# Turned u halves stored in 2 KB runs and put in order by GpSimd's product in the scans, and bf16 parts turned by TensorE

## The chip, the core and the metric

The kernel runs on one core of a Trainium2 chip. The time is the device time of one launch in microseconds (us), the median of three runs. Engines are named as in the profile: PE is TensorE's matmul (PEld its weight load), DVE is VectorE, ACT is ScalarE, POOL is GpSimd, and SP is SyncE, which here only issues DMAs.

## The reference

Two layers run over 8 images of 128 x 128 points with 128 channels. Layer 0 is linear attention with a layer norm and a residual. Layer 1 is a selective scan in four directions:

```
xb, z = split(x @ Win);  xb = silu(depthwise_conv3x3(xb) + b)          # 256 channels
xf = xb as rows;  xt = xb turned (H and W exchanged)
xs = [xf, reversed xf, xt, reversed xt]                                # u, four directions
dt, Bs, Cs = xs * Wxproj                                               # 8 + 1 + 1 rows
delta = softplus(dt_weight @ dt + bias);  h_l = exp(delta A) h_(l-1) + delta u B_l
y = sum over the directions of (h C_l + u D);  y = y silu(z);  out = norm(y) @ Wout
```

So the convolution's result is needed in two orders, natural and turned, and so are the ten rows of dt, B and C. A scan step needs the product of delta (softplus's result) and u B.

## The kernel before, in words

The launch has three parts, one after the other. Every part's instructions are written in the order in which each engine runs them (`in_order` chains all instructions of one engine, DMA issues on SP's and POOL's queues among them). A late instruction therefore holds up all that is written behind it on its engine.

**Layer 0** (up to about 2,360 us) is not touched by the change.

**layer1_front** (about 2,360 to 4,750 us) makes u. It runs over the images in the order 4, 6, 5, 7, 0, 1, 2, 3, and over each image in 16 steps of 1,024 points (eight lines). One step, `step(n)`, holds for both channel halves: the projection on PE (L478) and its copy by ACT (L487, edges L492), nine taps of the convolution (two on PE, L505; three as scaled copies on ACT, L513, which POOL adds up in two additions, L515; DVE adds the sum, L521, and does four taps, L523), SiLU on ACT into the tile `ures` (L530), the ten rows on PE (L539) and their copy (L543), B spread over the partitions by PE (L551), and the product of u and B on DVE (L560), stored to DRAM in natural order (L561). ACT and POOL sum u D over directions through the DRAM tiles `gts` and `gs` (L583, L586, L593, L605): images 0 and 1 read sums back and add them on POOL (L586), images 6, 7, 2, 3 issue two accumulating DMAs a step on POOL's queue (L605), images 4 and 5 only store.

The turned order comes from `ures`, eight steps later. `turn` (L617 or L627) copies 16 columns by 64 lines of `ures`, turned, into a tile `turned` (128 x 1,024 values); there are two copies a step, ka at the step's start and kb at its end, 256 in all. `copy_on` chooses the engine of each: DVE for 48 of them, by `dve_copy`, a scalar_tensor_tensor x * 1.0 max x that reads the tile twice (L627), POOL for 134, ACT for 69, and the tail's five plain copies on DVE. `store_turned` (L624) stores each to the DRAM tile `ubs[b, TURN]`. A full turned line has 128 values and the tile holds half of each, so a store has 2,048 runs of 256 B.

The ten rows of an image are loaded back two at a time during the next image (`load_rows`, L644), turned in fp32 by PE (L650) and copied by ACT (L652); both orders are then split into three bf16 parts each (`split`, which calls `split3`: three casts L44 and two subtractions L46; the casts on DVE are L627). The splits run on DVE while images 0 and 1 are in work, else on POOL. `store_parts` (L666) stores the parts to `xps`. After the last step a tail makes the last turned copies and splits.

**layer1_scan** (from 4,750 us) runs 8 groups of 4 slots of 16 units, 512 units of 1,024 points. Groups with o % 4 < 2 read the turned u, the others the natural one: 256 units each. One unit n, `step(n)`: `load_rows` (L934, L935) and `load` of u B for both channel halves (1 MB, L941), `delta` on PE (L952), `soften` on ACT (softplus from PSUM into `sp`, L956), `decay` on ACT (exp, L960), `weigh` on POOL (u B times softplus, in place in u's tile `ubt`, L963), `scan` on DVE (L971, L973, in place in `ubt`; its start value is the last column of the unit before), then `emit` on DVE (times C, L991, L994, L1001, L1005), `gather` on DVE (L1013) and `add` on POOL (two additions of 128 x 512, L1021). While a group's result leaves (slots 4, 8, 12 and so on of 32, and the end), the gate, norm and output projection run in between. `load(n + 3)` stands at the end of step n, because the tile it fills is free only then; `ubt` has four buffers of 8 KB a partition and `sp` two of 4 KB.

The lines that a sentence can't say, in the kernel before:

```
dst = ubs[b, TURN][c].rearrange("p (h w) -> p h w", w=W)
nc.sync.dma_start(dst[:, 16 * i : 16 * i + 16, hf * HALF : hf * HALF + HALF], turned.pop(k))
...
nc.gpsimd.tensor_tensor(ubt[n][:, c, :], ubt[n][:, c, :], sp.pop((n, c)), ALU.mult)
```

Of the kernel before, what the change touches and what calls it, by code (L numbers as in the profile page):

```python
# [8 lines left out]
F32 = mybir.dt.float32  # L9
# [28 lines left out]
NAT, TURN = 0, 1  # L38


def split3(eng, parts, x, copy):

    for j in range(3):
        copy(parts[j], x)  # L44
        if j < 2:
            eng.tensor_tensor(x, x, parts[j], ALU.subtract)  # L46

# [336 lines left out]
def layer1_front(ctx: ExitStack, tc, x1, win, conv_w, conv_b, wxp, d_par, ubs, xds, xps, gts, gs):  # L384
# [76 lines left out]
    def place_of(n):  # L461
        return SEQ[n // NCH % B], n % NCH
# [156 lines left out]
    def store_turned(k):  # L619
        m, r = divmod(k, COPIES)  # L620
        b, hf = SEQ[m // 2], m % 2
        c, i = divmod(r, COPIES // NC2)
        dst = ubs[b, TURN][c].rearrange("p (h w) -> p h w", w=W)
        nc.sync.dma_start(dst[:, 16 * i : 16 * i + 16, hf * HALF : hf * HALF + HALF], turned.pop(k))  # L624

    def dve_copy(out, x):
        nc.vector.scalar_tensor_tensor(out, x, 1.0, x, ALU.mult, ALU.max)  # L627

    def copy_on(n, second):
        s = place_of(n)[0] // 2 if n < N else 2  # L630
        if s == 0:
            return nc.scalar.copy if second else dve_copy if n % 2 else nc.gpsimd.tensor_copy
        if s % 2 == 1 and second:
            return dve_copy if n % 2 else nc.scalar.copy
        return nc.gpsimd.tensor_copy

    NROW = R + 2
    xws, parts = {}, []

    def load_rows(q, r0, rows, tag, bufs):  # L640
        x = wp.tile([P, rows, H], F32, name="xw", tag=tag, bufs=bufs)
        xws[q, r0] = x
        src = xds[SEQ[q]].rearrange("r (w h) -> w r h", h=H)
        nc.sync.dma_start(x, src[:, r0 : r0 + rows, :])  # L644

    def turn_rows(q, r0, rows, tag, bufs):
        x = xws[q, r0]
        pt = (pm if rows <= 4 else pj).tile([P, rows, P], F32, name="ptx", tag="m" if rows <= 4 else "pj")
        for j in range(rows):
            nc.tensor.transpose(pt[:, j, :], x[:, j, :], ident)  # L650
        y = wp.tile([P, rows, W], F32, name="xh", tag=tag, bufs=bufs)
        nc.scalar.copy(y, pt)  # L652
        xws[q, r0, TURN] = y

    def split(q, r0, rows, order, eng, tag, bufs):
        v = xws.pop((q, r0, TURN) if order == TURN else (q, r0))
        p = wp.tile([P, 3, rows, P], BF16, name="parts", tag=tag, bufs=bufs)
        split3(eng, [p[:, j] for j in range(3)], v, dve_copy if eng is nc.vector else eng.tensor_copy)
        parts.append((q, r0, rows, order, p))

    def store_parts():
        while parts:
            q, r0, rows, order, p = parts.pop()
            dst = xps[SEQ[q], order].rearrange("j r (a e) -> a j r e", e=P)
            for j in range(3):
                nc.sync.dma_start(dst[:, j, r0 : r0 + rows, :], p[:, j])  # L666

    def split_step(n):

        q, d = divmod(n - 2, NCH)  # L670
        q -= 1
        j, odd = divmod(d, 2)
        if not 0 <= q < B or n >= N or d > NROW:
            return
        eng = nc.vector if place_of(n)[0] // 2 == 0 else nc.gpsimd
        if odd:
            turn_rows(q, 2 * j, 2, "sy", 1)
            split(q, 2 * j, 2, NAT, eng, "sq", 1)
        else:
            if j:  # L680
                split(q, 2 * j - 2, 2, TURN, eng, "sq", 1)
            if 2 * j < NROW:
                load_rows(q, 2 * j, 2, "sx", 1)

    def step(n):

        live, then, later, before = 0 <= n < N, 0 <= n + 1 < N, 0 <= n + 2 < N, 1 <= n <= N
        b, g = place_of(n)
        ka, kb = 2 * (n - 8) - 1, 2 * (n - 8)
        if live:  # L690
            taps_dve(n, 0)
        if ka >= 0:
            turn(ka, copy_on(n, False), "tc", 2)
        if before:
            add_sum(n - 1)
        if before:
            keep_rows(n - 1)
        if live:
            taps_pe(n, 1)
        if later:  # L700
            load(n + 2)
        if then:
            project(n + 1, 1)
            taps_act(n + 1, 0)
            place(n + 1, 1)
        store_parts()
        if before:
            store_sum(n - 1)
        if live:
            for c in range(NC2):  # L710
                load_sum(n, c)
        if ka - 1 >= 0:
            store_turned(ka - 1)
        if before:
            for hf in range(2):
                spread(n - 1, hf)
        if live:
            silu(n, 0)
        if then:
            taps_pe(n + 1, 0)  # L720
        if later:
            project(n + 2, 0)
        if live:
            taps_dve(n, 1)
        if then:
            taps_act(n + 1, 1)
        if ka >= 0:
            store_turned(ka)
        if before:
            by_b(n - 1)  # L730
        if live:
            silu(n, 1)
        if later:
            place(n + 2, 0)
        if live:
            rows(n)
            sum_d(n)
        if kb >= 0:
            turn(kb, copy_on(n, True), "tc", 2)
        split_step(n)  # L740

    def tail():

        store_parts()
        q, k0 = B - 1, 2 * (N - 8)
        store_turned(k0)
        for i in range(2):
            load_rows(q, 5 * i, 5, "d", 2)
        for k in range(k0 + 1, 2 * B * COPIES):
# [2 lines left out]
            turn(k, copy, "tc" if i % 3 == 2 else "tb", 2 if i % 3 == 2 else 4)  # L752
            store_turned(k)
        for i in range(2):
            turn_rows(q, 5 * i, 5, "tb", 4)
            for order in (TURN, NAT):
                split(q, 5 * i, 5, order, nc.vector, "tb", 4)
                store_parts()

    with in_order(tc):  # L760
        for n in range(-2, N + 1):
# [5 lines left out]
def layer1_scan(ctx: ExitStack, tc, ubs, xps, zs, gs, dtw, dtb, a_log, gamma, beta, w_out, out):  # L767
# [34 lines left out]
    wparts = dram.tile([3, R, K, D2], BF16, name="wparts")  # L802
    bparts = dram.tile([3, K, D2], BF16, name="bparts")
    for dst, src, rows in ((wparts, dtw.rearrange("k r d -> r k d"), R), (bparts, dtb.rearrange("o (k d) -> o k d", d=D2), 1)):
        x = wp.tile([rows, K, D2], F32, name="w32", tag="sp", bufs=2)
        nc.sync.dma_start(x, src)
        q = wp.tile([rows, 3, K, D2], BF16, name="w16", tag="ub", bufs=4)
        split3(nc.vector, [q[:, j] for j in range(3)], x, nc.vector.tensor_copy)
        for j in range(3):
            if rows == 1:  # L810
                nc.sync.dma_start(dst[j : j + 1], q[:, j])
            else:
                nc.sync.dma_start(dst[j], q[:, j])
# [123 lines left out]
    def load(n):  # L937
        sl, i = units[n]
        m = sl.at(i)
        ubt[n] = wp.tile([P, NC2, CH], F32, name="ubt", tag="ub", bufs=4)  # L940
        nc.sync.dma_start(ubt[n], ubs[sl.b, sl.order].rearrange("c p l -> p c l")[:, :, m * CH : m * CH + CH])  # L941

    def delta(n, c):
        sl, i = units[n]
# [7 lines left out]
            nc.tensor.matmul(p[:, hf * 512 : hf * 512 + 512], sl.dw[:, c * P : c * P + P], src, start=True, stop=True)  # L952

    def soften(n, c):
        sp[n, c] = t = wp.tile([P, CH], F32, name="sp", tag="sp", bufs=2)
        nc.scalar.activation(t, da[n, c], AF.Softplus)  # L956

    def decay(n, c):
        sl, i = units[n]
        nc.scalar.activation(da[n, c], sp[n, c], AF.Exp, scale=sa[:, sl.s, c : c + 1])  # L960

    def weigh(n, c):
        nc.gpsimd.tensor_tensor(ubt[n][:, c, :], ubt[n][:, c, :], sp.pop((n, c)), ALU.mult)  # L963

    def scan(n, c):
        sl, i = units[n]
        x, e = da[n, c], ubt[n][:, c, :]
        last = 0 if sl.back else CH - 1
        start = 0.0 if i == 0 else ubt[n - 1][:, c, last : last + 1]
# [11 lines left out]
    def emit(n, hf):  # L981
# [1 line left out]


        sl, i = units[n]
        h = ubt[n][:, :, hf * 512 : hf * 512 + 512]
        c = cps.pop((n, hf)).to_broadcast([P, NC2, GN])
        if sl.place == 0:
            v = sl.y_at(i, hf)
# [25 lines left out]
    def add(n):  # L1015
        sl, i = units[n]
        hf = 1 - sl.first
        h = ubt[n][:, :, hf * 512 : hf * 512 + 512].rearrange("p c (a b) -> p c a b", b=H)
        v = sl.y_at(i, hf)
        for c in range(NC2):  # L1020
            nc.gpsimd.tensor_tensor(v[:, c], v[:, c], h[:, c], ALU.add)  # L1021
# [95 lines left out]
    def step(n):  # L1117
# [49 lines left out]
        if live:  # L1167
            scan(n, 1)
        if first:
            ubt.pop(n - 1)  # L1170
            if n + 3 < N:
                load(n + 3)
        if now:
            variance(now[1])
        if live:
# [16 lines left out]
            da.pop((n, 1))  # L1192
        if before and not first:
            add(n - 1)
            ubt.pop(n - 1)
        if n + 3 < N and not first:
            load(n + 3)
        if n in weighed:
            units[weighed[n]][0].weights()
        if n in summed:  # L1200
# [2 lines left out]
    with in_order(tc):  # L1203
        for n in range(2):
            units[n * NCH][0].weights()
        for n in range(2):
            load_rows(n)
        for n in range(3):
            load(n)
# [5 lines left out]
    assert not da and not ubt and not zt  # L1215


@with_exitstack
# [61 lines left out]
```

## Time and profile before

| | |
|---|---|
| median of three runs | 9462.86 us (9462.46 to 9480.5) |
| profiled execution | 9477.74 us; its span, first to last instruction, is 9475.9 us |
| layer 0, front, scans in that span | 0 to 2,360, 2,360 to 4,751, 4,751 to 9,476 us |
| busy shares over the span | DVE 86%, POOL 79%, ACT 75%, PE 67% |
| DMA | 1,784 MB in 1,510,245 packets, 799,444 of them under 512 B |

How to read the profile: a row of the group view names line, engine, operation, output <- inputs, the shapes and the count; behind the bar come busy time and the mean of one in ns, then the engine's idle time before the group and what ended it. The windows view gives each engine's busy time in a stretch with its instructions (x), and at the end of the row PE's granted clock, the share of time in which the 16 DMA engines were busy, and GB/s. "SPq" is SP's queue, where a row's time is that of the issue, not of the transfer.

### The profile page before, as it was taken

The page shows a single profiled execution, that of the slowest core. Times are in us where ns is not written, and L with a number is a line of the kernel's source. Part 1 is how long each engine was busy: PE and PEld are TensorE (multiplying, and loading weights), DVE is VectorE, ACT ScalarE, POOL GpSimd, SP SyncE. Part 2 cuts the span into 40 slices and gives each one's busy share as a digit, 9 for nine tenths or more (in the row PEclk, how much of TensorE's full clock was granted, in tenths as well). Part 3 has the DMA queues.
Part 4 walks back from the last instruction along what each step waited for, and adds up shares of the span by engine and source line. Part 5 has one row for each costly group of instructions (what it writes and reads, how often), then busy time and mean ns, then how long its engine had stood idle before and what let it go on. Part 6 is the DMA issues. An engine that isn't in the chain of part 4 may idle for free. (4 is left out here: it accounts for less than half of the span.)

```text
span 9475.9 us, 89695 instructions
## 1 busy us (share of the span) xinstructions
PE 6389.1 (67%) x24352; PEld 3122.5 (33%) x24352; DVE 8149.5 (86%) x8046; ACT 7125.4 (75%) x8034; POOL 7474.3 (79%) x4743
## 2 busy tenths in 40 slices
PE   8999999898989887788633644637345363543636
PEld 5555555564333332233200311304023040320403
DVE  6667765563999999999789999999999999999996
ACT  5556655567888887788678888888878888888884
POOL 3445544455789987788769999999999999999997
PEclk9999999999999998899855755758566585665857
DMA  2331233314598898999955958769586685967858
GB/s 92 134 134 71 106 134 132 133 63 152 180 230 244 231 231 229 233 232 224 226 158 171 273 154 228 223 181 264 158 238 203 190 256 166 247 187 201 248 163 214
DMA packets 1510245, 1784.08 MB, mean 188 GB/s; under 512 B 799444, under 2 KB 1025364, under 8 KB 1501552
## 3 DMA queue, kind: packets, MB, share of 16 engines
q1 hardware_dynamic: 1456496, 1577.01, 53.5%
q0 software_dynamic: 53248, 201.34, 11.4%
q8 instruction: 199, 3.26, 0.1%
q14 instruction: 302, 2.47, 0.1%
HBM read 1085.92 MB, written 692.12 MB: 188 GB/s over the span
## 5 line engine op out<-in xcount | busy, mean ns | idle before, releaser
L963 POOL TENSOR_TENSOR ubt<-ubt,sp 128x1024 f32<-128x1024 f32 x1024 | 2458.0, 2458 | 160.0 <-ACT sp L956 96.1
L952 PE MATMUL px<-rows,dtw 128*128 128x512 bf16 x2048 | 953.6, 565 | 2238.4 <-DVE y L1013 1069.2
L515 POOL TENSOR_TENSOR tap<-tap 128x1024 f32<-128x1024 f32 x512 | 1261.4, 2468 | 234.3 <-ACT tap L513 209.2
L523 DVE SCALAR_TENSOR_TENSOR acc<-xb,cw,acc 128x1024 f32<-128x1024 f32 x1024 | 1320.6, 1290 | 54.0 <-ACT xb L492 1.7
L956 ACT ACTIVATE sp<-px 128x1024 f32<-128x1024 f32 x1024 | 1046.2, 1024 | 418.1 <-PE px L952 351.0
L1021 POOL TENSOR_TENSOR y<-y,ubt 128x512 f32<-128x512 f32 x768 | 1155.3, 1550 | 146.0 <-DVE ubt L994 144.9
L505 PE MATMUL acc<-xi,wt 128*128 128x512 f32 x2048 | 1028.1, 648 | 314.3 <-ACT ures L530 314.3
L973 DVE TENSOR_TENSOR_SCAN ubt<-px,ubt 128x1024 f32<-128x1024 f32 x512 | 1176.9, 2332 | 27.4 <-POOL ubt L963 20.3
L971 DVE TENSOR_TENSOR_SCAN ubt<-px,ubt 128x1024 f32<-128x1024 f32 x512 | 1178.4, 2332 | 13.1 <-POOL ubt L963 6.0
L952 PEld LDWEIGHTS <-dtw 128*128 128x128 bf16 x2048 | 164.6, 109 | 3065.9 <-issue 869.7
L960 ACT ACTIVATE px<-sp,sa 128x1024 f32<-128x1024 f32 x1024 | 1110.1, 1109 | 6.1
L513 ACT ACTIVATE tap<-xb,cw 128x1024 f32<-128x1024 f32 x768 | 828.3, 1140 | 134.9 <-DVE acc L521 85.4
L282 POOL TENSOR_TENSOR q<-q,qs 128x512 f32<-128x512 f32 x256 | 271.7, 1061 | 698.2 <-DVE qs L281 698.2
L956 ACT ACT_TABLE_LOAD x512 | 656.9, 1283 | 169.6 <-PE px L952 146.9
L505 PEld LDWEIGHTS acc<-xi,wt 128*128 128x128 f32 x2048 | 398.1, 205 | 917.6 <-issue 497.1
L960 ACT ACT_TABLE_LOAD x512 | 656.9, 1283 | 9.0
L1086 PEld LDWEIGHTS px<-wg,z 128*128 128x128 f32 x4096 | 556.6, 219 | 117.9 <-issue 112.7
L979 PE MATMUL pc<-rows,csel 128*128 128x512 bf16 x1024 | 515.8, 584 | 81.3 <-DVE rstd L1074 77.5
L1086 PE MATMUL px<-wg,z 128*128 128x128 f32 x4096 | 556.7, 302 | 0.0
L478 PE MATMUL pxb<-xi,wi 128*128 128x512 f32 x1024 | 483.7, 595 | 10.1 <-DMA xi<-x 7.9
L1013 DVE TENSOR_TENSOR y<-y,px 128x1024 f32<-128x1024 f32 x384 | 468.7, 1221 | 14.4
L298 ACT ACTIVATE sq<-o 128x512 f32<-128x512 f32 x256 | 161.2, 630 | 420.1 <-DVE o L296 418.9
(160 smaller groups left out, 15379.7 us busy)
## 6 DMA issues: line engine op xcount, KB each, us to landing
ubt<-ubs SPq DMA_DIRECT2D x512, 1024.0 KB
zs<-z SPq DMA_DIRECT2D x512, 256.0 KB
ubs<-ures SPq DMA_DIRECT2D x256, 512.0 KB
ubs<-turned SPq DMA_DIRECT2D x256, 512.0 KB
z<-zs SPq DMA_DIRECT2D x256, 512.0 KB
y<-gs POOLq DMA_DIRECT2D x128, 1024.0 KB, 10.4
rows<-xps SPq DMA_DIRECT2D x1536, 60.0 KB
xi<-x SPq DMA_DIRECT2D x120, 576.0 KB
```

The lines of the kernel that those rows point to most:

```text
L505: nc.tensor.matmul(acc[:, s, :], wt[:, j, c, :], x, start=(j == 0), stop=(j == len(ON_PE) - 1))
L513: nc.scalar.activation(t, at(n, c, *d), AF.Copy, scale=cw[:, c, tap(*d) : tap(*d) + 1])
L515: nc.gpsimd.tensor_tensor(sums[n, c], sums[n, c], t, ALU.add)
L523: nc.vector.scalar_tensor_tensor(acc, at(n, c, *d), cw[:, c, tap(*d) : tap(*d) + 1], acc, ALU.mult, ALU.add)
L952: nc.tensor.matmul(p[:, hf * 512 : hf * 512 + 512], sl.dw[:, c * P : c * P + P], src, start=True, stop=True)
L956: nc.scalar.activation(t, da[n, c], AF.Softplus)
L960: nc.scalar.activation(da[n, c], sp[n, c], AF.Exp, scale=sa[:, sl.s, c : c + 1])
L963: nc.gpsimd.tensor_tensor(ubt[n][:, c, :], ubt[n][:, c, :], sp.pop((n, c)), ALU.mult)
L971: nc.vector.tensor_tensor_scan(e[:, ::-1], x[:, ::-1], e[:, ::-1], start, ALU.mult, ALU.add)
L973: nc.vector.tensor_tensor_scan(e, x, e, start, ALU.mult, ALU.add)
L1021: nc.gpsimd.tensor_tensor(v[:, c], v[:, c], h[:, c], ALU.add)
L1086: nc.tensor.matmul(po[:, w, :], z[:, c, w * H : w * H + H], wg[:, c, :], start=(c == 0), stop=(c == NC2 - 1))
```

## The change

Four edits.

1. `store_turned` writes the tile as it lies: a chunk of 1,024 points of `ubs[b, TURN]` now holds two half blocks (columns 0 to 63 of eight lines, then columns 64 to 127), each one run of 2 KB. A store has 256 runs of 2 KB in place of 2,048 of 256 B.
2. `weigh` multiplies from `ubt` into softplus's tile `sp`; for turned units it reads `ubt` by a view of 8 lines by 2 halves by 64 columns, which restores the order. `scan`, `emit` and `add` then work in `sp`, which becomes three buffers of both halves (8 KB), while `ubt` becomes four buffers of one half (4 KB); `load(n + 2, c)` is issued per half, right behind `weigh(n, c)`.
3. The rows are split first (natural order only) and the three bf16 parts are turned by PE (six transposes with a bf16 identity in place of two fp32 ones), copied by ACT and stored.
4. No copy or split of the steps runs on DVE: the 48 copies go to POOL (134 to 170) and ACT (69 to 81), and all splits but the tail's to POOL. A copy on ACT stands at the end of the step; a copy on POOL stands where ka and kb stood.

```
-        dst = ubs[b, TURN][c].rearrange("p (h w) -> p h w", w=W)
-        nc.sync.dma_start(dst[:, 16 * i : 16 * i + 16, hf * HALF : hf * HALF + HALF], turned.pop(k))
+        dst = ubs[b, TURN][c].rearrange("p (g e q) -> p g e q", e=2, q=8 * HALF)[:, 2 * i : 2 * i + 2, hf, :]
+        nc.sync.dma_start(dst, turned.pop(k).rearrange("p (g h) w -> p g (h w)", g=2))
...
         if s == 0:
-            return nc.scalar.copy if second else dve_copy if n % 2 else nc.gpsimd.tensor_copy
-        if s % 2 == 1 and second:
-            return dve_copy if n % 2 else nc.scalar.copy
-        return nc.gpsimd.tensor_copy
+            late = n % 2 == 0 if second else n % 8 != 0
+        else:
+            late = s % 2 == 1 and second and n % 2 == 1
+        return nc.scalar.copy if late else nc.gpsimd.tensor_copy
...
+    def split(q, r0, rows, eng, tag, bufs):
+        p = wp.tile([P, 3, rows, P], BF16, name="parts", tag=tag, bufs=bufs)
+        split3(eng, [p[:, j] for j in range(3)], xws[q, r0])
+        xws[q, r0] = p
+        parts.append((q, r0, rows, NAT, p))
+
+    def turn_parts(q, r0, rows, tag, bufs):
+        p = xws.pop((q, r0))
+        pt = (pm if rows <= 2 else pj).tile([P, 3, rows, P], BF16, name="ptx", tag="m" if rows <= 2 else "pj")
+        for j in range(3):
+            for r in range(rows):
+                nc.tensor.transpose(pt[:, j, r, :], p[:, j, r, :], ident16)
+        y = wp.tile([P, 3, rows, P], BF16, name="xh", tag=tag, bufs=bufs)
         nc.scalar.copy(y, pt)
+        parts.append((q, r0, rows, TURN, y))
...
-        eng = nc.vector if place_of(n)[0] // 2 == 0 else nc.gpsimd
         if odd:
-            turn_rows(q, 2 * j, 2, "sy", 1)
-            split(q, 2 * j, 2, NAT, eng, "sq", 1)
+            split(q, 2 * j, 2, nc.gpsimd, "sq", 1)
         else:
             if j:
-                split(q, 2 * j - 2, 2, TURN, eng, "sq", 1)
+                turn_parts(q, 2 * j - 2, 2, "sy", 1)
...
     def soften(n, c):
-        sp[n, c] = t = wp.tile([P, CH], F32, name="sp", tag="sp", bufs=2)
-        nc.scalar.activation(t, da[n, c], AF.Softplus)
+        if c == 0:
+            sp[n] = wp.tile([P, NC2, CH], F32, name="sp", tag="sp", bufs=3)
+        nc.scalar.activation(sp[n][:, c, :], da[n, c], AF.Softplus)
...
     def weigh(n, c):
-        nc.gpsimd.tensor_tensor(ubt[n][:, c, :], ubt[n][:, c, :], sp.pop((n, c)), ALU.mult)
+        u, t = ubt.pop((n, c)), sp[n][:, c, :]
+        if units[n][0].order == TURN:
+            u = u.rearrange("p (e h w) -> p h e w", e=2, w=W // 2)
+            t = t.rearrange("p (h e w) -> p h e w", e=2, w=W // 2)
+        nc.gpsimd.tensor_tensor(t, u, t, ALU.mult)
...
             weigh(n, 0)
+            if n + 2 < N:
+                load(n + 2, 0)
...
             weigh(n, 1)
+            if n + 2 < N:
+                load(n + 2, 1)
```

More of the change, by code (lines that the diff above doesn't have):

```diff
@@ L38, with split3 @@
 NAT, TURN = 0, 1
-def split3(eng, parts, x, copy):
+def split3(eng, parts, x):
     for j in range(3):
-        copy(parts[j], x)
+        eng.tensor_copy(parts[j], x)
         if j < 2:
@@ L412, in layer1_front @@
     make_identity(nc, ident)
+    ident16 = const.tile([P, P], BF16, name="ident16")
+    nc.vector.tensor_copy(ident16, ident)
     cw = const.tile([P, NC2, 9], F32, name="cw")
@@ L622, in store_turned @@
         c, i = divmod(r, COPIES // NC2)
-        dst = ubs[b, TURN][c].rearrange("p (h w) -> p h w", w=W)
-        nc.sync.dma_start(dst[:, 16 * i : 16 * i + 16, hf * HALF : hf * HALF + HALF], turned.pop(k))
-    def dve_copy(out, x):
-        nc.vector.scalar_tensor_tensor(out, x, 1.0, x, ALU.mult, ALU.max)
+        dst = ubs[b, TURN][c].rearrange("p (g e q) -> p g e q", e=2, q=8 * HALF)[:, 2 * i : 2 * i + 2, hf, :]
+        nc.sync.dma_start(dst, turned.pop(k).rearrange("p (g h) w -> p g (h w)", g=2))
     def copy_on(n, second):
@@ L640, in load_rows @@
     def load_rows(q, r0, rows, tag, bufs):
-        x = wp.tile([P, rows, H], F32, name="xw", tag=tag, bufs=bufs)
-        xws[q, r0] = x
+        xws[q, r0] = x = wp.tile([P, rows, H], F32, name="xw", tag=tag, bufs=bufs)
         src = xds[SEQ[q]].rearrange("r (w h) -> w r h", h=H)
         nc.sync.dma_start(x, src[:, r0 : r0 + rows, :])
[L646 to L651, printed above, removed]
-        nc.scalar.copy(y, pt)
[L653 to L659, printed above, removed]
+    def split(q, r0, rows, eng, tag, bufs):
[10 more added lines that the diff above has]
+        y = wp.tile([P, 3, rows, P], BF16, name="xh", tag=tag, bufs=bufs)
+        nc.scalar.copy(y, pt)
+        parts.append((q, r0, rows, TURN, y))
     def store_parts():
         while parts:
-            q, r0, rows, order, p = parts.pop()
+            q, r0, rows, order, p = parts.pop(0)
             dst = xps[SEQ[q], order].rearrange("j r (a e) -> a j r e", e=P)
@@ L691, in step @@
             taps_dve(n, 0)
-        if ka >= 0:
-            turn(ka, copy_on(n, False), "tc", 2)
+        late = []
+        for k, second in ((ka, False), (kb, True)):
+            if k >= 0 and copy_on(n, second) == nc.scalar.copy:
+                late.append(k)
+        if ka >= 0 and ka not in late:
+            turn(ka, nc.gpsimd.tensor_copy, "tc", 2)
         if before:
@@ L711, in step @@
                 load_sum(n, c)
-        if ka - 1 >= 0:
-            store_turned(ka - 1)
+        for k in sorted(turned):
+            if k != ka:
+                store_turned(k)
         if before:
@@ L726, in step @@
             taps_act(n + 1, 1)
-        if ka >= 0:
+        if ka in turned:
             store_turned(ka)
@@ L737, in step @@
             sum_d(n)
-        if kb >= 0:
-            turn(kb, copy_on(n, True), "tc", 2)
+        for k in (ka, kb):
+            if k in late:
+                turn(k, nc.scalar.copy, "tc", 2)
+            elif k == kb >= 0:
+                turn(k, nc.gpsimd.tensor_copy, "tc", 2)
         split_step(n)
@@ L745, in tail @@
         q, k0 = B - 1, 2 * (N - 8)
-        store_turned(k0)
+        for k in sorted(turned):
+            store_turned(k)
         for i in range(2):
@@ L754, in tail @@
         for i in range(2):
[L755 to L758, printed above, removed]
+            split(q, 5 * i, 5, nc.vector, "tb", 4)
+            turn_parts(q, 5 * i, 5, "tb", 4)
+        store_parts()
     with in_order(tc):
@@ L804, in layer1_scan @@
     for dst, src, rows in ((wparts, dtw.rearrange("k r d -> r k d"), R), (bparts, dtb.rearrange("o (k d) -> o k d", d=D2), 1)):
-        x = wp.tile([rows, K, D2], F32, name="w32", tag="sp", bufs=2)
+        x = wp.tile([rows, K, D2], F32, name="w32", tag="sp", bufs=3)
         nc.sync.dma_start(x, src)
-        q = wp.tile([rows, 3, K, D2], BF16, name="w16", tag="ub", bufs=4)
-        split3(nc.vector, [q[:, j] for j in range(3)], x, nc.vector.tensor_copy)
+        q = wp.tile([rows, 3, K, D2], BF16, name="w16", tag="sp", bufs=3)
+        split3(nc.vector, [q[:, j] for j in range(3)], x)
         for j in range(3):
@@ L935, in load_rows, with load @@
         nc.sync.dma_start(rw[96:99, :], xps[sl.b, sl.order, :, R + 1, m * CH : m * CH + CH])
-    def load(n):
+    def load(n, c):
         sl, i = units[n]
         m = sl.at(i)
-        ubt[n] = wp.tile([P, NC2, CH], F32, name="ubt", tag="ub", bufs=4)
-        nc.sync.dma_start(ubt[n], ubs[sl.b, sl.order].rearrange("c p l -> p c l")[:, :, m * CH : m * CH + CH])
+        ubt[n, c] = wp.tile([P, CH], F32, name="ubt", tag="ub", bufs=4)
+        nc.sync.dma_start(ubt[n, c], ubs[sl.b, sl.order, c][:, m * CH : m * CH + CH])
     def delta(n, c):
@@ L954, in soften @@
     def soften(n, c):
-        sp[n, c] = t = wp.tile([P, CH], F32, name="sp", tag="sp", bufs=2)
-        nc.scalar.activation(t, da[n, c], AF.Softplus)
+        if c == 0:
+            sp[n] = wp.tile([P, NC2, CH], F32, name="sp", tag="sp", bufs=3)
+        nc.scalar.activation(sp[n][:, c, :], da[n, c], AF.Softplus)
     def decay(n, c):
         sl, i = units[n]
-        nc.scalar.activation(da[n, c], sp[n, c], AF.Exp, scale=sa[:, sl.s, c : c + 1])
+        nc.scalar.activation(da[n, c], sp[n][:, c, :], AF.Exp, scale=sa[:, sl.s, c : c + 1])
     def weigh(n, c):
-        nc.gpsimd.tensor_tensor(ubt[n][:, c, :], ubt[n][:, c, :], sp.pop((n, c)), ALU.mult)
+        u, t = ubt.pop((n, c)), sp[n][:, c, :]
[3 more added lines that the diff above has]
+        nc.gpsimd.tensor_tensor(t, u, t, ALU.mult)
     def scan(n, c):
         sl, i = units[n]
-        x, e = da[n, c], ubt[n][:, c, :]
+        x, e = da[n, c], sp[n][:, c, :]
         last = 0 if sl.back else CH - 1
-        start = 0.0 if i == 0 else ubt[n - 1][:, c, last : last + 1]
+        start = 0.0 if i == 0 else sp[n - 1][:, c, last : last + 1]
         if sl.back:
@@ L985, in emit @@
         sl, i = units[n]
-        h = ubt[n][:, :, hf * 512 : hf * 512 + 512]
+        h = sp[n][:, :, hf * 512 : hf * 512 + 512]
         c = cps.pop((n, hf)).to_broadcast([P, NC2, GN])
@@ L1017, in add @@
         hf = 1 - sl.first
-        h = ubt[n][:, :, hf * 512 : hf * 512 + 512].rearrange("p c (a b) -> p c a b", b=H)
+        h = sp[n][:, :, hf * 512 : hf * 512 + 512].rearrange("p c (a b) -> p c a b", b=H)
         v = sl.y_at(i, hf)
@@ L1169, in step @@
         if first:
-            ubt.pop(n - 1)
-            if n + 3 < N:
-                load(n + 3)
+            sp.pop(n - 1)
         if now:
@@ L1194, in step @@
             add(n - 1)
-            ubt.pop(n - 1)
-        if n + 3 < N and not first:
-            load(n + 3)
+            sp.pop(n - 1)
         if n in weighed:
@@ L1207, in layer1_scan @@
             load_rows(n)
-        for n in range(3):
-            load(n)
+        for n in range(2):
+            for c in range(NC2):
+                load(n, c)
         for c in range(NC2):
@@ L1214, in layer1_scan @@
             step(n)
-    assert not da and not ubt and not zt
+    assert not da and not ubt and not sp and not zt
 @with_exitstack
```

## The prediction

> **What bounds the kernel now.** I read the windows view first, one row per image of the front, then two slots of the scans, to see which engine is full in which stage. Layer 0 (to 2,360 us) is untouched.
>
> ```profile
> core 0: us, PE busy (x) PEld busy (x) DVE busy (x) ACT busy (x) POOL busy (x), PEclk, DMA share, GB/s
> 2381.00:2626.00 245.00, 227.90 (x568) 87.49 (x568) 235.16 (x190) 219.82 (x239) 181.87 (x84) 0.99 0.61 195
> 2626.00:2906.00 280.00, 241.03 (x595) 92.60 (x592) 260.46 (x201) 236.55 (x254) 247.91 (x167) 0.97 0.94 229
> 2906.00:3156.00 250.00, 230.10 (x580) 88.79 (x578) 238.34 (x193) 217.22 (x240) 236.63 (x152) 0.99 0.83 249
> ...
> 3445.00:3779.00 334.00, 251.52 (x574) 96.86 (x572) 316.69 (x251) 243.90 (x251) 268.19 (x107) 0.88 0.90 232
> ...
> 5028.00:5160.00 132.00, 46.46 (x97) 10.86 (x96) 129.71 (x82) 108.62 (x97) 125.49 (x65) 0.50 0.57 176
> 5293.00:5472.00 179.00, 142.59 (x978) 101.22 (x971) 169.06 (x215) 145.69 (x158) 162.94 (x88) 0.92 0.94 277
> ```
>
> DVE is fullest everywhere. Images 4 and 5 (rows 1 and 3) have no turned copy on DVE and take 245 and 250 us, 15.3 to 15.6 a step. Image 6 (row 2) has DVE copies in its odd steps and takes 280; images 7, 2, 3 take 289, 291, 282. Image 0 (row 4), with the splits on DVE too, takes 334, image 1 338. The group view of image 6 and the timeline around a copy show why:
>
> ```profile
> L523 DVE SCALAR_TENSOR_TENSOR acc<-xb,cw,acc 128x1024 f32<-128x1024 f32 x128 | 165.1, 1290 | 6.6
> L521 DVE TENSOR_TENSOR acc<-tap,acc 128x1024 f32<-128x1024 f32 x32 | 39.1, 1221 | 0.0
> L560 DVE TENSOR_TENSOR ures<-ures,pb 128x1024 f32<-128x1024 f32 x33 | 38.7, 1214 | 0.0
> L627 DVE SCALAR_TENSOR_TENSOR turned<-ures 128x1024 f32<-128x1024 f32 x8 | 23.4, 2920 | 13.0 <-DMA ubs<-turned 13.0
> ```
>
> A copy costs DVE 2.9 us and, on average over these eight, 1.6 us of waiting for the store that frees its tile. Those stores are the many small packets:
>
> ```profile
> DMA packets 108837, 64.10 MB, mean 229 GB/s; under 512 B 76202, under 2 KB 95786, under 8 KB 108823
> ```
>
> In the scans an ordinary unit takes 132/16 = 8.2 us, with DVE at 98% and POOL at 95%. The timeline shows DVE going from scan to emit without a gap and POOL about 2.5 us ahead of it:
>
> ```profile
> 5069.15 4.58 DVE L973 TENSOR_TENSOR_SCAN ubt<-px,ubt 128x1024 f32<-128x1024 f32 x2
> 5069.31 3.22 POOL L1021 TENSOR_TENSOR y<-y,ubt 128x512 f32<-128x512 f32 x2 [0.40 <-DVE ubt L994]
> ```
>
> **The front, by engine and step (16 steps an image), after the change.**
>
> DVE: 8 x 1.290 + 2 x 1.222 + 2 x 1.214 = 15.2 us, in every image. Copies and splits are gone from it.
>
> ACT without copies: 6 taps x 1.140 (L513) + 2 x 1.109 (L530) + 2 x 1.007 (L487) + 2 x 0.407 (L492) + 0.572 (L543) + 2 x 1.140 (L583, L593) = 14.74. A copy is 1.99 (L617). The copy of turned parts reads 128x768; the rows 355 ns at 128x256 and 692 at 128x640 (L652) give 0.8 us, five an image, 0.25 a step. Images 6, 7, 2, 3 copy in every second step: 14.74 + 1.0 + 0.25 = 16.0. Images 0 and 1 make 44 copies in 32 steps: 14.74 + 2.74 + 0.25 = 17.7.
>
> POOL: four additions x 2.41 (L515, third image) = 9.64. A natural split is 3 x 0.40 + 2 x 0.67 = 2.54 us (L44, L46), five an image, 0.79 a step; the turned splits vanish. A copy is 2.00 (L617). Images 6, 7, 2, 3: 9.64 + two DMA issues 2.03 (L605) + 1.5 copies 3.0 + 0.79 = 15.5. Images 0 and 1: 9.64 + 2 x 2.88 (L586) + 10/16 x 2.0 + 0.79 = 17.4. Image 5: 9.64 + 4.0 + 0.79 = 14.4.
>
> PE: 36 matmuls a step as now, plus bf16 transposes in place of fp32 ones: 240 for 80 over the whole front. The nearest rows, 300 ns for an fp32 transpose (L650), bound the 160 extra at 48 us over 128 steps beside PE's idle 7 to 25%; I take nothing.
>
> DMA: in the packet records of image 6 a 256 B packet holds an engine for 18 ns and a 2 KB packet for 84 to 89. A turned store thus falls from 2,048 x 18 / 16 = 2.3 us of all 16 engines to 256 x 89 / 16 = 1.4, or 1.8 us less a step. Image 6's DMA work of 0.94 x 17.5 = 16.4 a step becomes 14.7, image 0's 0.90 x 20.9 = 18.8 becomes 17.0. Both stay under ACT, image 0 barely.
>
> So ACT becomes the fullest engine, at 16.0 and 17.7 us, with DVE and POOL close behind. A stage does not reach its fullest engine's sum. Against the sums of DVE's durations now, image 4 takes 1% over 15.2, image 5 3%, images 0 and 1 3 to 4.5% over 20.2 (15.2, eight copies of 3.2 an image and five double splits of some 11 us), and image 6 5% over 16.65 (15.2 and eight copies of 2.92), store waits included. I take 3.5%: 16.55 x 16 = 265 for images 6, 7, 2, 3; 18.35 x 16 = 294 for 0 and 1; 247 for image 5; 245 for image 4. The sum is 4 x 265 + 2 x 294 + 247 + 245 = 2,140 against 2,309 (2,381 to 4,690): **-170 us**. At 1% it would be -211, at 6.5% -120. Moving the copies to ACT is free only while DVE's slack covers it: ACT's late copies stand ahead of L543's copy of the rows, for which PE's spread of B (L551) and then DVE's L560 wait, 2 us later in images 0 and 1. DVE needs that at the end of its step, so several us of cover remain.
>
> **Tail.** From 4,690 us to the first scan at 4,783 SP issues 15 turned stores in one 35 us row (2.3 us each, which is the packet price), then DVE makes 20 split operations of 0.82 us. The stores shrink by 15 x 0.9 = 13 us. Ten split operations go (8 us); transposes and two copies of 128x1920 (1.8 us each by the same line) add about 4. I take **-15**, bounds -6 (stores no faster) and -24.
>
> **Scans.** DVE's operations are the same, in other tiles. Three sp buffers let softplus of unit n+1 start once `add(n-2)` is done, one step earlier than needed; ACT's softplus waits for PSUM now (L956 on PE px L952, 337 us in this stage), so nothing follows. The loads move from the end of scan n to behind `weigh(n)`, and are needed two units later: about 14 us of lead in place of 15, against some 6 us from the first load's issue to POOL's first product. The new waits stand on SP's queue; behind them stand the stores of r and the next unit's rows, and weigh(n) ends before the scan that both follow, so I cost that at nothing. The first product waits for half a load: -2.
>
> The product's new view is not in the trace. Below, it could cost nothing more, and nothing in the change makes it cheaper than today's 2.37 us. Above, L586 reads one operand with a 32 B step: 2.88 against 2.37, +0.51; worse is the addition L1021 in turned slots, 1.62 against 1.26 per 512 values, +0.73 per 1,024, with two operands at 512 B steps. Nearest is L282: 16 runs of 32 values beside a broadcast take 1.05 per 512, no more than the plain 1.26. The new view has runs of 64, so I take 0.
>
> [...]
>
> **Sum.** -170 - 15 - 2 = -187 on the profiled execution's 9477.7, so 9290. The median lies 15 below that execution; the forecast is 9290 - 15 = 9275.
>
> **Rivals.**
> - The three full engines couple worse, as copies come in bursts (up to 4 us of ACT's time in an even step of images 0 and 1): 10% over the fullest sum, 17.6 and 19.5 a step, front -64, in all about 9380. For it: ACT, POOL, DMA and DVE are all within 2 us. Against: image 5 runs at 3% with POOL at 95%.
> - The stores are no cheaper in 2 KB runs (the change doesn't do what it says): DMA stays at 0.94, so 17.5 a step in images 6, 7, 2, 3, and 18.8 / 0.94 = 20 in 0 and 1; -28, tail -6: 9430. Against: the 2 KB packets' own 84 ns.
> - The product costs +0.51, as L586. An ordinary unit has 0.35 us of POOL's time left, the units of leaving slots about 1.0, slot 0 more. 12 ordinary turned slots x 16 x (1.02 - 0.35) + little in three leaving ones = 130: 9405.
> - **Slower**: the product is priced like the turned addition, +0.73. POOL then bounds the turned units: 192 x (1.46 - 0.35) + 48 x (1.46 - 1.0) = 235 us against 187 saved, 9275 + 235 = 9510. It decides where 480 products' extra less 115 us of slack eats the 187, at +0.63, a product of about 3.0 us.
>
> **How the numbers follow.** Forecast 0.72 (own range 9208 at 1%, tail -24 and 20 more from SP's shorter queue; 9337 at 6.5% and tail -6); coupling 0.10; stores 0.05; product +0.51 0.06; slower 0.07. The range reaches to the coupling case: 9205 to 9385, which leaves out 0.18. A measurement of this kernel tells about 0.2% (19 us) from no change; 9430 is 33 under, so part of that case counts as same: faster 0.90, same 0.03, slower 0.07.
>
> **What would show it.** Right: images 6, 7, 2, 3 at 260 to 270 us and 0 and 1 at 285 to 300, ACT above 95% there; packets under 512 B down by 524,288; the tail row of stores near 21 us; the product at 2.37 us in turned slots and an ordinary unit at 8.2. Wrong: DVE idle for PE acc L505 behind ACT (coupling), a DMA share still at 0.94, or turned slots longer than natural ones.

## The result and the profile after

The changed kernel takes 10,189.99 us (median of four runs, 10,178.22 to 10,196.01) where the kernel before takes 9,468.54 on the same chip: 1.0759 times as long, 95% interval 1.074 to 1.0777. The profiled execution took 10,178.22 us, its span is 10,176.4.

| us | before | after | forecast | measured |
|---|---|---|---|---|
| layer 0, to the front's first tap | 2,381 | 2,374 | 0 | -7 |
| front | 2,309 | 2,284 | -170 | -26 |
| tail | 93 | 72 | -15 | -21 |
| scans | 4,693 | 5,447 | -2 | +754 |

The front begins with DVE's first work on an image and ends with its last product of u and B; the scans run from the first scan to the span's end. Layer 0 is untouched: over all the traces here it differs by some 10 us. The windows view of after, with rows for images 4, 6, 5 and 0, the slot of the scans ahead of the first one in which a group leaves, and that leaving slot:

```profile
2374.00:2620.00 246.00, 228.91 (x570) 87.88 (x570) 235.32 (x191) 219.91 (x239) 181.82 (x85) 0.99 0.56 195
2620.00:2894.00 274.00, 235.13 (x600) 89.26 (x596) 239.00 (x192) 231.64 (x250) 237.01 (x149) 0.98 0.85 228
2894.00:3145.00 251.00, 234.10 (x610) 90.99 (x610) 239.12 (x194) 223.08 (x245) 226.65 (x128) 0.99 0.74 254
3421.00:3756.00 335.00, 262.96 (x607) 99.42 (x608) 240.51 (x193) 263.93 (x267) 267.56 (x136) 0.89 0.84 236
5182.00:5335.00 153.00, 47.39 (x105) 11.98 (x109) 131.35 (x80) 108.80 (x97) 128.72 (x76) 0.50 0.72 187
5335.00:5549.00 214.00, 167.31 (x985) 122.78 (x978) 161.78 (x216) 148.24 (x159) 148.95 (x88) 0.78 0.82 232
```

The slot ahead of the leaving one, before:

```profile
5160.00:5293.00 133.00, 47.03 (x103) 11.19 (x107) 129.22 (x81) 109.89 (x98) 127.29 (x75) 0.50 0.79 211
```

Read the rows against those of before. In image 6 DVE's work fell from 260 to 239 us and the DMA share from 0.94 to 0.85, as the change meant them to, but the image lost only 6 us: now PE, DVE, ACT and POOL are all at 85 to 87%. In image 0 DVE fell from 317 to 241 and the image did not get shorter at all. In the slot of the scans DVE and POOL have nearly the work they had, yet it grew from 133 to 153 us and both stand idle for 14 to 16% of it. (A slot with no work of a leaving group beside it grew from 131.5 to 151.2; the seven leaving slots grew from 180 to 215 on average, 245 of the 754 us.) Where every engine has room and the time is still spent, one suspects a chain that closes from one step to the next.

The group view names the first such chain:

```profile
L974 POOL TENSOR_TENSOR sp<-ubt,sp 128x1024 f32<-128x1024 f32 x1024 | 2393.5, 2358 | 1179.7 <-ACT px L967 555.9
...
L984 DVE TENSOR_TENSOR_SCAN sp<-px,sp 128x1024 f32<-128x1024 f32 x512 | 1191.3, 2345 | 406.1 <-POOL sp L974 406.0
```

POOL's product takes 2.36 us (2.46 before), in natural and turned slots alike, so the new view costs nothing. But POOL stands idle for 1,180 us ahead of it, 556 of them until ACT's exp (L967), and the scans wait for the product for 406 + 399 us (26 before). The timeline of one unit shows the loop (rows between left out; a row's idle time stands in brackets):

```profile
5266.67 4.66 DVE L984 TENSOR_TENSOR_SCAN sp<-px,sp 128x1024 f32<-128x1024 f32 x2 [1.08 <-POOL sp L974]
...
5269.08 1.03 PE L958 MATMUL px<-rows,dtw 128*128 128x512 bf16 x2 [3.56 <-DVE sp L984]
...
5270.15 1.02 ACT L963 ACTIVATE sp<-px 128x1024 f32<-128x1024 f32 x1 [2.24 <-PE px L958]
...
5271.19 1.28 ACT L967 ACT_TABLE_LOAD   x1
...
5272.49 2.15 ACT L967 ACTIVATE px<-sp,sa 128x1024 f32<-128x1024 f32 x2
...
5273.75 2.34 POOL L974 TENSOR_TENSOR sp<-ubt,sp 128x1024 f32<-128x1024 f32 x1 [1.24 <-DMA rows<-xps]
```

The row of scans is two of 2.33 us. The first ends at 5269.0 and frees a PSUM buffer (`px`, which PE writes); PE fills it for the next unit, ACT makes softplus, loads exp's table and makes two exps; the product starts 0.16 us after the first exp's end (5272.49 + 1.10), and the next scan starts with the product's end, at 5276.12: 9.45 us a unit, and 16 x 9.45 = 151. The exp reads `sp`, and the product now writes `sp`, so it may not start until that exp has read. Before, the product wrote into `ubt`, and exp and product both only read softplus's tile. The bracket's releaser ("rows<-xps") is inferred; the times say more. In after none of the 1,024 products starts before the exp of its tile has ended; in before 1,023 of them did, by 3.1 us in the median.

### The profile page after: what moved, and what is told of

The parts are those of the page before. It is cut to its first block, busy times and chain, and to the rows that moved or that the text cites. A ratio compares the mean times of both kernels' runs of the same rounds, so it can differ in the third digit from the quotient of the medians.

```text
span 10176.4 us, 89797 instructions
## 1 busy us (share of the span) xinstructions
PE 6528.0 (64%) x24512; PEld 3233.5 (32%) x24512; DVE 7907.9 (78%) x7889; ACT 7150.0 (70%) x8046; POOL 7323.3 (72%) x4704
## 5 line engine op out<-in xcount | busy, mean ns | idle before, releaser
L974 POOL TENSOR_TENSOR sp<-ubt,sp 128x1024 f32<-128x1024 f32 x1024 | 2393.5, 2358 | 1179.7 <-ACT px L967 555.9
L958 PE MATMUL px<-rows,dtw 128*128 128x512 bf16 x2048 | 981.5, 580 | 2927.8 <-DVE y L1024 1022.7
L963 ACT ACTIVATE sp<-px 128x1024 f32<-128x1024 f32 x1024 | 1047.2, 1023 | 945.3 <-PE px L958 939.9
L984 DVE TENSOR_TENSOR_SCAN sp<-px,sp 128x1024 f32<-128x1024 f32 x512 | 1191.3, 2345 | 406.1 <-POOL sp L974 406.0
L982 DVE TENSOR_TENSOR_SCAN sp<-px,sp 128x1024 f32<-128x1024 f32 x512 | 1192.5, 2345 | 399.0 <-POOL sp L974 398.7
L517 POOL TENSOR_TENSOR tap<-tap 128x1024 f32<-128x1024 f32 x512 | 1212.8, 2371 | 276.5 <-ACT tap L515 256.2
L1032 POOL TENSOR_TENSOR y<-y,sp 128x512 f32<-128x512 f32 x768 | 1150.2, 1529 | 0.0
L967 ACT ACTIVATE px<-sp,sa 128x1024 f32<-128x1024 f32 x1024 | 1109.9, 1109 | 6.1
L1097 PEld LDWEIGHTS px<-wg,z 128*128 128x128 f32 x4096 | 623.5, 240 | 84.2 <-issue 74.7
L1097 PE MATMUL px<-wg,z 128*128 128x128 f32 x4096 | 616.1, 322 | 0.0
L990 PE MATMUL pc<-rows,csel 128*128 128x512 bf16 x1024 | 547.0, 615 | 31.0 <-DVE rstd L1085 25.9
L523 DVE TENSOR_TENSOR acc<-tap,acc 128x1024 f32<-128x1024 f32 x256 | 313.8, 1226 | 292.4 <-PE acc L507 190.1
L480 PE MATMUL pxb<-xi,wi 128*128 128x512 f32 x1024 | 488.4, 599 | 48.5 <-DMA xi<-x 46.4
```

The lines of the kernel that those rows point to most:

```text
L517: nc.gpsimd.tensor_tensor(sums[n, c], sums[n, c], t, ALU.add)
L963: nc.scalar.activation(sp[n][:, c, :], da[n, c], AF.Softplus)
L967: nc.scalar.activation(da[n, c], sp[n][:, c, :], AF.Exp, scale=sa[:, sl.s, c : c + 1])
L974: nc.gpsimd.tensor_tensor(t, u, t, ALU.mult)
L984: nc.vector.tensor_tensor_scan(e, x, e, start, ALU.mult, ALU.add)
L1097: nc.tensor.matmul(po[:, w, :], z[:, c, w * H : w * H + H], wg[:, c, :], start=(c == 0), stop=(c == NC2 - 1))
```

## The experiments

Each expectation was written before its run. The theory HAZARD: the product's write into softplus's tile costs the scans their 750 us. Its rivals: the view, the loads, and the front's parts.

**own_tile.** After's front and loads; the product gets a tile of its own, `pr`.

```
-        sp[n] = wp.tile([P, NC2, CH], F32, name="sp", tag="sp", bufs=3)
+        sp[n, c] = t = wp.tile([P, CH], F32, name="sp", tag="sp", bufs=2)
...
+        pr[n] = wp.tile([P, NC2, CH], F32, name="pr", tag="pr", bufs=2)
...
-        nc.gpsimd.tensor_tensor(t, u, t, ALU.mult)
...
+        nc.gpsimd.tensor_tensor(e, u, t, ALU.mult)
```

> The changed kernel, but the product of u and softplus goes to a tile of its own (two buffers of both halves, 8 KB each; softplus keeps two of one half, 4 KB, as in the kernel before; u's four halves and the place of their loads stay as changed). Theory HAZARD: the product written into softplus's tile must wait until exp (decay) has read that tile, so ACT's exp, POOL's product and DVE's scan became one chain of 9.45 us a unit. It expects ordinary units back at 8.2 us, the scans back from 5,447 to about 4,690 us, and 9,435 in all (10,190 less 754). Rival LOADS: u's loads per half, now behind the product on SP's queue, and the rows' loads behind them, come too late; they stay where they are, so units stay at 9.45 and the total near 10,190. Rival LAYOUT: the half-block layout and the product's view slow the scans: units stay at 9.45 in the turned slots.

Measured: 9,476.73 us, ratio to before 1.0012 (1.0002 to 1.0022); scans 4,750. 697 of the 754 us are gone with the write moved; the buffers changed with it (softplus has its two half tiles again), while the loads stayed where after has them, so LOADS falls. The group view's line of the product:

```profile
L976 POOL TENSOR_TENSOR pr<-ubt,sp 128x1024 f32<-128x1024 f32 x1024 | 2417.8, 2392 | 364.7 <-DMA rows<-xps 92.8
```

The exp is no longer what mostly ends its wait, and its idle time fell from 1,180 to 365 us. A slot that takes 131.5 us in before takes 131.5 again, and the view is still in it, so LAYOUT falls too. The total is some 40 us above what I expected: 56 us of the scans and nearly all of the front's missing gain were left to explain.

**sp_only.** Before's front with after's scan, but without the turned view (u stored in full order).

```
-        nc.gpsimd.tensor_tensor(ubt[n][:, c, :], ubt[n][:, c, :], sp.pop((n, c)), ALU.mult)
+        u, t = ubt.pop((n, c)), sp[n][:, c, :]
+        nc.gpsimd.tensor_tensor(t, u, t, ALU.mult)
...
```

> The kernel before with one part of the change alone: the product goes to softplus's tile (three buffers of both halves), u's loads per half behind it; stores, copies, splits and the natural view of u are those of the kernel before. Theory HAZARD: scans at about 5,447 us, 10,220 in all. Rival LOADS expects the same here (own_tile tells it apart). Rival LAYOUT: no half blocks here, so scans at 4,690 and 9,468 in all.

Measured: 10,248.31 us (one run), scans 5,457. The whole loss comes back without the view, the turned store or the new front. HAZARD stands.

**copies_back.** own_tile with before's 48 copies on DVE and its places.

```
-            late = n % 2 == 0 if second else n % 8 != 0
...
+            return nc.scalar.copy if second else dve_copy if n % 2 else nc.gpsimd.tensor_copy
...
```

> own_tile with the turned copies on the engines and at the places of the kernel before (48 on DVE by the doubled read, ACT's not moved to the step's end); 2 KB stores, splits on POOL and bf16 turning stay. It is for the front, 2,284 us after the change against 2,309 before, where 2,140 were forecast. Theory COPIES: ACT's late copies and POOL's copies that wait for a tile whose store stands later on SP's queue give back what DVE gained. It expects images 6, 7, 2, 3 at about 272 us (274 to 285 after), images 0 and 1 at about 285 (335 and 337 after), front about 2,155 and 9,305 in all. Rival TRANSFERS: the DMA engines or the issue of the stores bound the step; then the front stays at about 2,280, and DVE's copies make it no shorter: 9,435.

Measured: 9,428.12, ratio 0.9962 (0.9947 to 0.9977). Images 0 and 1 take 304 and 311 (own_tile 325 and 338), images 6, 7, 2, 3 take 281, 282, 287, 285 (own_tile 272, 274, 280, 287). COPIES, which named 285 and 272 for these two groups and a front of 2,155, is wrong: images 6, 7 and 2 became some 8 us longer, and the front takes 2,238. Images 0 and 1 gained 48 us, and 37 of them lie in three steps that stall in own_tile (see early_store). In image 0 the DMA share rose to 0.89, so the transfers did not hold own_tile at 0.86. The total is near what TRANSFERS named, but not for its reason.

**runs_only.** own_tile's scans with before's front, in which only the layout of the turned store is new (2 KB runs).

```
...
-        nc.sync.dma_start(dst[:, 16 * i : 16 * i + 16, hf * HALF : hf * HALF + HALF], turned.pop(k))
...
+        nc.sync.dma_start(dst, turned.pop(k).rearrange("p (g h) w -> p g (h w)", g=2))
```

> The kernel before with the 2 KB stores and the product's view and own tile (as own_tile) alone: copies, splits and fp32 turning are those of the kernel before. It prices the stores. If the small packets' waits were the price of image 6's odd steps, images 6, 7, 2, 3 fall from 280 to 291 to about 272, images 0 and 1 stay above 320 (the splits are on DVE), the tail loses 10 to 15 us: front about 2,240, 9,385 in all. If the stores are no cheaper to the step in 2 KB runs: 9,450 to 9,470.

Measured: 9,504.26, ratio 1.004 (1.0025 to 1.0055). Front 2,303 (before 2,309), tail 76 (before 93). Image 6's DMA share fell to 0.81 and the image takes 282 us as before (280). Cheaper stores alone move only the tail. The total lies above both cases because own_tile's scans come with it: they take 4,747 here, 54 more than before.

So the front needed a theory. The timeline of ACT in image 6 of after, from one SiLU of the first half (L532) to the next, and of PE beside it:

```profile
2747.05 1.11 ACT L532 ACTIVATE ures<-acc,cb 128x1024 f32<-128x1024 f32 x1
...
2755.11 1.02 ACT L489 COPY xb<-pxb 128x1024 f32<-128x1024 f32 x1 [2.83 <-PE pxb L480]
...
2758.56 1.96 ACT L619 COPY turned<-ures 128x1024 f32<-128x1024 f32 x1
...
2765.37 1.11 ACT L532 ACTIVATE ures<-acc,cb 128x1024 f32<-128x1024 f32 x1
...
2773.20 1.01 ACT L489 COPY xb<-pxb 128x1024 f32<-128x1024 f32 x1 [2.60 <-PE pxb L480]
...
2782.28 1.11 ACT L532 ACTIVATE ures<-acc,cb 128x1024 f32<-128x1024 f32 x1
```

```profile
2766.53 3.70 PE L507 MATMUL acc<-xi,wt 128*128 128x512 f32 x8 [2.56 <-ACT ures L532]
2771.20 1.96 PE L480 MATMUL pxb<-xi,wi 128*128 128x512 f32 x4 [0.97 <-DMA xi<-x]
```

PE waits 2.6 us for ACT's SiLU to free `acc`, then makes its taps and the projection; ACT meanwhile runs dry and waits 2.6 us for that projection. LOOP: the step is this round trip, some 15.4 us (image 4's 246 over 16 steps), and everything that ACT does between the projection's copy (L489) and the next SiLU lies on it, the copy of 1.96 us (L619) too. The step with the copy takes 18.3 us, the next one 16.9. The 0.97 us ahead of L480 stand in the round trip as well: there PE waits for the load of its input, 12.5 us in image 6 of after (1.2 in before).

A second stall shows in images 0 and 1: at every eighth step POOL copies `ka` and waits for a tile whose store is issued late. POOL's and SP's timelines of after there:

```profile
3608.63 1.89 POOL L619 COPY turned<-ures 128x1024 f32<-128x1024 f32 x1 [11.27 <-issue]
```

```profile
3598.78 3.59 SPq L576 DMA_DIRECT2D gl<-gts  x2
3602.42 8.49 SPq L626 DMA_DIRECT2D ubs<-turned  x3
```

Three such steps take 32.5, 29.3 and 32.5 us, and the same or 0.1 less in own_tile. QUEUE: they wait because the store stands behind other work on SP's queue.

**early_store.** own_tile, with those tiles stored at the step's start.

```
+        if n % 8 == 0 and b // 2 == 0:
+            for k in sorted(turned):
+                store_turned(k)
```

> The kernel own_tile with one line more: in images 0 and 1, at every eighth step, the turned tiles still waiting are stored at the step's start, ahead of POOL's copy ka, where SP had their store further down its queue. In after's trace three such steps take 32.5, 29.3 and 32.5 us in place of some 20, with POOL idle for 11.3 us ahead of the copy (L619) and DVE 16.5 us behind POOL's tap. QUEUE (those steps wait for a store that stands behind other work on SP's queue): the three steps fall by 11 to 14 us each, images 0 and 1 from 325 and 338 to about 312, the whole from 9,477 to about 9,437. TRANSFERS (the tile comes free late because the DMA engines are full, wherever the store stands): no change, 9,470 to 9,480.

Measured: 9,457.57, ratio 0.9986 (0.9976 to 0.9996). The three steps fell to 21.3, 19.6 and 21.3, so 32 us in all, and QUEUE is right about them, TRANSFERS wrong; but the step behind each of them, which had caught up at 15.3, now takes 18.4 to 20.6, and images 0 and 1 gained only 4 and 11 us, so QUEUE's total is missed by 20. Of the 32 us, 13 were given back in the very next steps. A third buffer for that tile was not tried.

**mid_copies.** own_tile with ACT's copies right behind SiLU, where ACT waits; only ACT's second copies in images 0 and 1 stay at the step's end.

```
-            late = s % 2 == 1 and second and n % 2 == 1
+            late = s % 2 == 1 and not second and n % 2 == 1
...
         if live:
             silu(n, 0)
+        if ka in late:
+            turn(ka, nc.scalar.copy, "tc", 2)
...
```

> The kernel own_tile with ACT's copies elsewhere: ACT makes ka, right behind SiLU of the first half, where ACT waits for PE (35 us an image), in place of kb at the step's end; POOL makes the others at their old places. Images 6, 7, 2, 3: one copy on ACT in odd steps as before, but early. Images 0, 1: ka of seven steps in eight early, kb of even steps at the end. LOOP (a step's length is ACT's and PE's chain from SiLU to SiLU, about 15.4 us and each late copy's 2 us on top): the early copy falls into ACT's wait, images 6, 7, 2, 3 go from 272 to 287 down to 256 to 262, images 0 and 1 from 325 and 338 to 300 to 310 and the stalls of every eighth step; in all about 9,390. WORK (ACT's sum, or the transfers', bounds the step, wherever the copy stands): no change, 9,470 to 9,480.

Measured: 9,382.74, ratio 0.9905 (0.9888 to 0.9922); front 2,177 against own_tile's 2,272. Images 6, 7, 2, 3 take 267, 265, 271, 265, images 0 and 1 310 and 306. As many copies on the same engines, in other places, are worth 95 us, with the DMA share higher than in own_tile: WORK falls. The 95 are not all LOOP's: 44 of them lie in images 6, 7, 2 and 3, 5 in image 5 and 46 in images 0 and 1, where the three stalled steps also fell from 94 to 63 us. POOL's copy of the odd steps moved to the step's end in exchange; in own_tile's image 6 DVE had waited 25.3 us for PE's taps and 0.7 for POOL, so POOL's place did not matter there. The four images stay 3 to 9 us above the upper end of what LOOP named. In image 6 PE still waits 9.3 us for loads and ACT 4.4 for a store; that these waits are the missing 5 us is not shown. Its windows view, images 6 and 0, and ACT's timeline:

```profile
2626.00:2893.00 267.00, 238.67 (x602) 90.71 (x599) 238.81 (x193) 234.72 (x250) 235.20 (x149) 0.97 0.85 236
3405.00:3715.00 310.00, 252.21 (x608) 96.47 (x609) 239.87 (x193) 262.22 (x265) 267.86 (x136) 0.93 0.89 255
```

```profile
2749.23 1.11 ACT L532 ACTIVATE ures<-acc,cb 128x1024 f32<-128x1024 f32 x1
2750.24 1.99 ACT L619 COPY turned<-ures 128x1024 f32<-128x1024 f32 x1
...
2757.54 1.02 ACT L489 COPY xb<-pxb 128x1024 f32<-128x1024 f32 x1 [1.19 <-PE pxb L480]
...
2766.08 1.11 ACT L532 ACTIVATE ures<-acc,cb 128x1024 f32<-128x1024 f32 x1
...
2777.31 1.15 ACT L595 ACTIVATE du<-ures,sd 128x1024 f32<-128x1024 f32 x1 [2.10 <-DMA gts<-du]
...
2783.99 1.11 ACT L532 ACTIVATE ures<-acc,cb 128x1024 f32<-128x1024 f32 x1
```

ACT's wait for the projection shrank from 2.8 to 1.2 us and the step with a copy takes 16.9. The next one takes 17.9, with 2.1 us of waiting for the store that frees `du`.

**mixed.** Images 6, 7, 2, 3 as in mid_copies, 0 and 1 as in copies_back.

> Images 6, 7, 2, 3 as in mid_copies; images 0 and 1 as in copies_back (ka on DVE in odd and on POOL in even steps at the step's start, kb on ACT at the end); the rest is own_tile. By LOOP the four images take 256 to 262 and images 0 and 1 the 304 and 311 of copies_back: 9,428 less some 95, about 9,335. By WORK images 6, 7, 2, 3 take own_tile's 272 to 287: about 9,415. If a copy in the middle of a step delays the first tap of the next and with it DVE, they take over 287: over 9,428.

Measured: 9,374.29, ratio 0.9894 (0.9875 to 0.9913). Images 6, 7, 2, 3: 261, 264, 272, 276; images 0 and 1: 308 and 304. The total lies between the cases, 39 us above LOOP's; mid_copies' own placement in images 0 and 1 is as good.

**gate_late.** This is for the 56 us left in own_tile's scans. The group view shows DVE's gate slower there than in after (1.78 us in before):

```profile
L1052 DVE TENSOR_TENSOR z<-y,z 128x1024 f32<-128x1024 f32 x120 | 150.3, 1253 | 0.0
```

```profile
L1054 DVE TENSOR_TENSOR z<-y,z 128x1024 f32<-128x1024 f32 x120 | 256.2, 2135 | 0.0
```

The first line is after's, the second own_tile's. The kernel is mixed with the gate behind both emits, where a product is further along.

```
-        if now and last:
-            gate(*now, 1, nc.vector)
         if before:
             emit(n - 1, 1 - half1)
+        if now and last:
+            gate(*now, 1, nc.vector)
```

> The kernel mixed with DVE's gate (z times y, 120 of them, in the slots in which a group leaves) behind both emits of its step in place of between them. Own_tile's scans are 55 us longer than before's; in its trace the gate takes 2.14 us beside POOL's product, 1.78 in before and 1.25 in after, where POOL stands idle then: 42 us of the 55. In mixed the gate starts 1.1 us after a product of 2.4 us; behind the emits it starts 2.3 us after it, when the product is over. PRODUCT (the gate is slowed by POOL's product alone): it takes 1.25 to 1.5 us, 80 to 110 us less in all, the seven leaving slots some 12 to 15 us shorter each, the whole about 9,270 to 9,300. POOL (any work of POOL slows it, the small operations on rstd behind the product too): it stays at 2.1 us, and as ACT's square, which waits for it, then holds up the second exp, the whole is at 9,374 or above, up to 9,500.

Measured: 9,365.79, ratio 0.9891 (0.9874 to 0.9909), the lowest median of all, though its interval and mixed's overlap. Its gate:

```profile
L1055 DVE TENSOR_TENSOR z<-y,z 128x1024 f32<-128x1024 f32 x120 | 183.5, 1529 | 0.0
```

The gate fell from mixed's 2.16 to 1.53 us, 75 us in all, close to PRODUCT's figure, though 87 of the 120 gates still start before a product is over. The other 33, some of them beside POOL's small operations on rstd, take 1.22 us: POOL falls. But PRODUCT's total is missed by 66 us: the scans fell only from 4,740 to 4,727. DVE's waits took the rest: for the store that frees tile `r` (L1106) from 55 to 88 us, for ACT's exp from 5 to 26. So the gate's price is real and mostly not on the bound. What sets the other 34 us against before's 4,693 stays open; they lie in the seven leaving slots (182.4 us on average against 179.6) and in the slots ahead of them (135.2 against 133.2).

## Why the prediction was wrong

**Scans, -2 forecast, +754 measured: the step that failed.** It said "Three sp buffers let softplus of unit n+1 start once `add(n-2)` is done, one step earlier than needed; ACT's softplus waits for PSUM now (L956 on PE px L952, 337 us in this stage), so nothing follows", and "The new waits stand on SP's queue". It asked who may write a buffer again, not who still reads the tile that the product is now written into, and so put the wait at nothing. The exp (L967) does read it, and the wait stands on POOL's queue. The slot's own rows gave the price: PE, softplus, table, exp, product and scan add up to 9.1 us, 9.45 with the hand-offs, in place of 8.2, where POOL had run 2.5 us ahead of DVE. No rival held this: the slower one put the price on the view, which costs nothing. own_tile and sp_only show it from both sides.

**Front, -170 forecast, -26 measured.** The parts were right: DVE without copies 14.9 us busy a step, the copy 1.96 to 1.99 us on ACT and POOL, the parts' copy 0.78, the DMA engines' work 14.6 and 17.6 us a step (14.7 and 17.0 forecast). What failed is "ACT becomes the fullest engine ... I take 3.5%" with "several us of cover remain". ACT, which the forecast wanted above 95% there, is busy 14.5 us of image 6's 17.1, or 85%: successive activations overlap by 0.1 us in the profile (three of 1.14 end after 3.23), so a sum of durations is too long. It waits for PE 37 us in that image. In images 6, 7, 2 and 3, which miss their forecast by 54 us together, the bound is ACT's and PE's round trip, on which the late copies lie: not the 16.0 of a full engine, but the 15.4 of image 4, which makes no copy on ACT, plus what stands in the loop. Images 0 and 1 miss theirs by 84; the stalled steps hold some 30 of that, the rest is not taken apart: even in mid_copies they take 310 and 306 where 294 was forecast. The rival "coupling" came nearest in size (17.6 and 19.5 a step; measured 17.1 to 17.8 and 20.9 to 21.1) but named bursts of copies, not a loop, and got a chance of 0.10. The rival of unchanged stores was mispriced: its own steps give about -55 us for the front, not -28. With the copies out of the loop images 6, 7, 2, 3 do reach 265 to 271.

The prediction's sign of coupling, DVE idle for PE's taps behind ACT, did come true: 10.5 us before, 190.1 after. In the group views of before and of after:

```profile
L521 DVE TENSOR_TENSOR acc<-tap,acc 128x1024 f32<-128x1024 f32 x256 | 312.9, 1222 | 32.8 <-POOL tap L515 22.4 <-PE acc L505 10.5
```

```profile
L523 DVE TENSOR_TENSOR acc<-tap,acc 128x1024 f32<-128x1024 f32 x256 | 313.8, 1226 | 292.4 <-PE acc L507 190.1 <-POOL tap L517 93.7 <-POOL du L588 7.9
```

**Transfers.** Packets under 512 B fell by 516,096 (the 524,288 of 256 B that were forecast, less 8,192 new ones of 4 B), the share in image 6 to 0.85, the tail's 15 stores to 18.9 us of SP's time (1.26 each; the forecast said 21). The term was right; with the stores alone changed, runs_only gained 17 us in the tail and 6 in the front.

In after's image 6 the fullest engine is DVE at 87%, with PE, POOL and ACT at 85 to 87%, and DVE's own work was not the lever: 95 us of own_tile's front, which is built like after's, came from moving copies without changing any engine's work.

## What to carry to other kernels

An in-place destination is a wait for every other reader of that tile (here one, ACT's exp, and 697 us of the scans): list them, with their engines and queues, before an output is moved into a tile that "is free anyway". When no engine is full (85 to 87% here), look for two engines that wait for each other once a step; work is then priced by its place in that loop and not by its engine's sum, and ACT's idle time behind a SiLU was worth 44 us in four images as a place for copies. A stall found in one step must be weighed with the step behind it: 32 us of stalls paid 15.

## What the runs showed of the hardware

DVE's gate, a product of two SBUF tiles, takes 1.21 or 1.22 us in 113 of its 120 cases in after, where none starts while POOL's product runs, and ends later where that product runs when it starts. One such pair in mixed's timelines, DVE's and POOL's:

```profile
5214.56 2.35 DVE L1055 TENSOR_TENSOR z<-y,z 128x1024 f32<-128x1024 f32 x1
```

```profile
5213.45 2.37 POOL L977 TENSOR_TENSOR pr<-ubt,sp 128x1024 f32<-128x1024 f32 x1 [1.33 <-ACT mv L1084]
```

POOL ends at 5215.82; the gate's end, 5216.91, is 1.1 us later, nearly a whole gate. So it is in all 98 such pairs of mixed: the gate ends 1.08 or 1.09 us after the product, as it does in all 85 of before. The emits and scans, which read one operand from PSUM, keep their 1.22 and 2.33 us beside the same product: in before the 904 emits that start while one runs take 1.22 us on average, the 116 scans 2.34. The gate's row above has no idle time in brackets and 2.35 us of busy time, so in the group view the delay shows as a longer mean alone (2.16 us in mixed, 1.25 in after).
